# Where the feed-forward of a two-layer kernel turns its next block's tokens: behind a block's first products instead of behind its second ones

## The chip, the core and the metric

The kernel runs on one core of one Trainium2 chip. A core has a matrix engine (TensorE, PE in the profile), three engines for elementwise work (VectorE or DVE, ScalarE or ACT, GpSimd or POOL), a queue that issues transfers (SyncE, SP), and an accumulator memory (PSUM) from which the other engines must fetch what PE has made. Each engine works its own instructions in the order in which they were built, and waits on semaphores for the others. The metric is the time of one execution on the device in microseconds (us).

## The reference, cut to what matters

Tokens are 4 sequences of 1024, each of width 256. Two layers are computed; each has a mixing part and a feed-forward part, each followed by a residual and a layer norm:

```
x = layernorm(x + L0_attn(x))      # state-space mixing, 2 heads of 128
x = layernorm(x + gelu(x @ w1 + b1) @ w2 + b2)   # w1 256x1024, w2 1024x256, exact gelu
x = layernorm(x + L1_attn(x))      # linear attention: exp features of q and k, 16 heads
x = layernorm(x + L1_ffn(x))       # 2 shared experts and 2 of 8 routed experts, silu
```

The change lies in the second line. Its first product makes the 1024 hidden values of a token, its second one brings them back to 256.

## The kernel before, in words

The tokens are cut into 8 blocks (`i`) of 512, each of 4 tiles of 128. All data is float32. A block goes through the state-space part (`ssd_block`), the feed-forward (`ffn_block`), attention and the router in halves of 256 tokens (`attn_front`, `attn_back`, index `hb`, two for each block; `attn_tail`), the shared experts (`shared_jobs`, run as `job`), and last the routed experts (`slot_tiles`), which come after everything else.

**The order on PE is planned while the program is built.** Each stage registers pieces of work as `Task(run, cost, rank, after, pool, banks, hold)`. `trace_tasks` then simulates a single server: again and again it takes the task that can start first, and among those that can start at once the one of lowest rank. A task starts no sooner than `wait` units after the tasks in `after`, and no sooner than its `banks` of PSUM are free in its pool. Pool 0 has six banks and pool 1 has two. The planner's costs are constants in the code. What it writes down is an order of instructions, and the hardware then keeps that order on PE, whatever the waits really last. ACT and DVE get an order that follows from it. While attention, feed-forward and shared experts overlap, low ranks (attention, near 5) go before high ones (feed-forward, 10 and more; shared experts, 100).

**The feed-forward of one block** is nine tasks in pool 1. `turn_x` transposes the block's tokens on PE into two banks; ACT copies both to `xT` (tile of one buffer). `hidden`, four tasks, makes two of the eight slices of hidden values each: four matmuls (eight records in the profile) into two banks, then a GELU for each bank on ACT into `hT` (also one buffer). `outputs`, four tasks for the four tiles, multiplies `hT` with `w2`; each pair shares one bank, and one addition on DVE takes the pair into the residual. The last one is followed by the layer norm. In front of the first, POOL adds the bias `b2` to the residual.

Blocks are taken in the order 0, 2, 1, 3, 4, 5, 6, 7. Each is chained behind the one before: `turn_x` waits until the last `outputs` of the preceding block has been placed (`before`).

**What shares the engines with it.** From block 1 on, attention runs in between. `attn_front` transposes its tokens (`turn_x` of its own, one copy on ACT to `xTa`), makes queries and keys (`project`), transposes these (`turn_qk`, for keys a copy on ACT to `qkT`, for queries one on DVE), and makes the features (`features`, first of the keys, then of the queries): PE fills four banks, and ACT and DVE clip and exponentiate them: two clips on DVE, two relus on ACT (L583), four exponentials on ACT (L581, L584). `attn_back` has `scores` (one ACT copy, a multiplication on POOL, three on DVE), `turn_keys` (two ACT copies to `kt`), `outputs`, `turn`, `turn_back` (ACT copy to `oT`) and `project`. The exponentials, the GELU and the SiLU of the shared experts belong to different function tables of ACT; a table is changed by an instruction ACT_TABLE_LOAD ahead of the next function.

When the last block's `outputs` are done, `open_second` gives the space of the feed-forward's weights to those of the shared experts and loads them; 20 units later the first shared `job` may start. All `job`s use pool 1 while attention runs.

Of the kernel before, what the change touches and what calls it, by code (L numbers as in the profile page):

```python
# [76 lines left out]
def two_layers(ctx: ExitStack, tc: tile.TileContext, x, xT, vecs, cols, wx, w1, w2, wqkv, wout, om, rw, moe, out):  # L77
# [19 lines left out]
    def bank(name, n):  # L97

        return psum[n].tile([P, 512], F32, tag="bank", name=name)
# [100 lines left out]
    def transposed(t, i, tiles, n, engines):  # L200


        width = len(tiles) * P
        engines = list(engines)
        for c0 in range(0, KC, 512 // width):
            chunks = range(c0, min(KC, c0 + 512 // width))
            ps = bank(f"ps_t{t.name}_{c0}", n)
            at = 0
            for c in chunks:
                for j in tiles:  # L210
                    nc.tensor.transpose(ps[:, at : at + P], xs[i][:, j, c * P : (c + 1) * P], ident)
                    at += P
            engines.pop(0)(t[:, c0 : chunks[-1] + 1, :].rearrange("p c t -> p (c t)"), ps[:, :at])
        return t

    def layernorm(i, by_act=False):

        st = sm.tile([P, NT, 6], F32, tag="ln_st", name=f"ln_st{i}")
        mv = sm.tile([P, NT, 2], F32, tag="ln_mv", name=f"ln_mv{i}")
        v = sm.tile([P, NT], F32, tag="ln_v", name=f"ln_v{i}")  # L220
        for j in range(NT):
            nc.vector.bn_stats(st[:, j, :], xs[i][:, j, :])
            nc.vector.bn_aggr(mv[:, j, :], st[:, j, :])
        nc.vector.tensor_scalar_add(v, mv[:, :, 1], LN_EPS)
        r = rsqrt(v, [P, NT], "ln")
        if by_act:
            nc.vector.scalar_tensor_tensor(v, mv[:, :, 0], -1.0, r, ALU.mult, ALU.mult)
            for j in range(NT):
                nc.scalar.activation(
                    xs[i][:, j, :], xs[i][:, j, :], AF.Identity, bias=v[:, j : j + 1], scale=r[:, j : j + 1]  # L230
                )
            return
        for j in range(NT):
            nc.vector.tensor_scalar(
                xs[i][:, j, :], xs[i][:, j, :], mv[:, j, 0:1], r[:, j : j + 1], ALU.subtract, ALU.mult
            )
# [37 lines left out]


    states = [None] * NB
    ssd_end, ffn_end, proj_end, turn_end, tail_end = {}, {}, {}, {}, {}

    def ssd_block(i, wk):

# [153 lines left out]
    def ffn_block(i, before, wk):  # L434
        v = SimpleNamespace(ps=None)

        def turn_x():
            v.xT = wk.tile([P, KC, TB], F32, tag="xT", name=f"xT{i}")
            transposed(v.xT, i, range(NT), 1, (nc.scalar.copy, nc.scalar.copy))
            v.hT = wk.tile([P, HID0 // P, TB], F32, tag="hT", name=f"hT{i}")  # L440

        def hidden(ms):
            for m in ms:
                ps = bank(f"ps_h{i}_{m}", 1)
                for k in range(KC):
                    nc.tensor.matmul(  # L446
                        ps, w1_sb[:, k, m * P : (m + 1) * P], v.xT[:, k, :], start=(k == 0), stop=(k == KC - 1)
                    )
                nc.scalar.activation(v.hT[:, m, :], ps, AF.Gelu, bias=col[:, m : m + 1])  # L449

        def outputs(j):
            if j == 0:
                b2 = vec0[:, _VEC["b2"]].unsqueeze(1).to_broadcast([P, NT, D])
                nc.gpsimd.tensor_add(xs[i], xs[i], b2)
            if j % 2 == 0:
                v.ps = bank(f"ps_f{i}_{j}", 1).rearrange("p (s d) -> p s d", s=2)
            for m in range(HID0 // P):
                nc.tensor.matmul(  # L458
                    v.ps[:, j % 2, :],
                    v.hT[:, m, j * P : (j + 1) * P],  # L460
                    w2_sb[:, m, :],
                    start=(m == 0),
                    stop=(m == HID0 // P - 1),
                )
            if j % 2 == 1:
                nc.vector.tensor_add(xs[i][:, j - 1 : j + 1, :], v.ps, xs[i][:, j - 1 : j + 1, :])
            if j == NT - 1:
                layernorm(i)

        r = 10.0 + i  # L470
        last = Task(turn_x, 0.9, r, [(ssd_end[i], 10.0), (before, 0.0)], 1, 2)
        wait = 4.0
        for n in range(4):
            last = Task(lambda n=n: hidden(range(2 * n, 2 * n + 2)), 3.5, r + 0.1 * n, [(last, wait)], 1, 2, 2.2)
            wait = 0.0
        wait = 3.0
        for j in range(NT):
            last = Task(lambda j=j: outputs(j), 3.5, r + 0.5 + 0.1 * j, [(last, wait)], 1, (j + 1) % 2, 2.2)
            wait = 0.0
        ffn_end[i] = last  # L480
# [676 lines left out]
    with tc.manual_schedule(engines={mybir.EngineType.PE}):  # L1157
# [8 lines left out]
        before = None  # L1166
        ffn_order = [0, 2, 1, 3, 4, 5, 6, 7]
        for i in ffn_order:
            ffn_block(i, before, wkf)
            before = ffn_end[i]  # L1170
        constants = Task(attn_constants, 0.0, 4.0, [(ssd_end[0], 0.0)])
        spaces = SimpleNamespace()

# [32 lines left out]
        last = Task(open_second, 0.0, 0.0, [(ffn_end[ffn_order[-1]], 0.0)])  # L1206
        wait, jobs = 20.0, []
        for i, _, cost, n, banks, _ in shared_jobs(early + amid, None, None, None, banks_of, 2):
            after = [(last, wait), (turn_end[i], 3.0)]
# [3 lines left out]
            last, wait = jobs[-1], 0.0  # L1213
# [31 lines left out]
        wait = 6.0  # L1245
        for _ in range(2 * NTOK // P // 8 + 1):
            sending = Task(lambda: spaces.steps.pop(0)(), 0.0, 0.0, [(sending, wait)])
            wait = 3.6
# [14 lines left out]
    with tc.manual_schedule(  # L1263
# [7 lines left out]
        parts, n = [], -1  # L1271
# [94 lines left out]
```

## Time and profile before

| | |
|---|---|
| median of 3 runs | 1563.77 us (1562.93 to 1565.25) |
| profiled execution, its own time | 1563.55 us |
| its span, first to last instruction | 1561.7 us |
| PE clock that was granted, mean | 0.987 of full |
| VectorE busy | 754.3 us (48%) |
| ScalarE busy | 595.6 us (38%) |
| GpSimd busy | 419.6 us (27%) |
| first feed-forward matmul of block 1 (the first beside attention) | 188.1 us |
| weights of the shared experts issued | 661.3 us |
| first product of the shared experts | 686.8 us |
| first product of the routed experts | 1063.9 us |

The span is 1.85 us shorter than the execution's own time; what lies around it is taken to stay. Matmuls in float32 show as two records each. A row of the timeline gives start, duration, engine, source line, output and inputs, the number of records, and in brackets the idle time ahead of it with the instruction that ended it. A row of the windows gives, for a stretch of time, the length, the busy time of PE, weight loads, DVE, ACT and POOL with their instruction counts, the granted clock, and the share and rate of the transfers.

### The profile page before, as it was taken

What the parts mean: (1) busy time and instruction counts of PE and PEld (TensorE: products, weight loads), DVE (VectorE), ACT (ScalarE), POOL (GpSimd) and SP (SyncE); (2) the same over time, 40 slices, a digit from 0 to 9 for tenths busy, and PEclk for the clock granted to TensorE, in tenths of its full rate; (3) what the DMA queues carried; (4) which work ended last, traced back from release to release, by engine and by line L of the source; (5) the groups of instructions that cost most, each with busy time, mean ns of one, the idle gap of its engine ahead of it and who ended that gap; (6) DMA issues with size and microseconds to landing.
All of it is one profiled execution on the core that took longest, in us unless ns stands there. A gap on an engine that the chain in (4) does not pass through costs nothing. (4 is left out here: it accounts for less than half of the span.)

```text
span 1561.7 us, 25308 instructions
## 1 busy us (share of the span) xinstructions
PE 1492.0 (96%) x9704; PEld 966.5 (62%) x9704; DVE 754.3 (48%) x2322; ACT 595.6 (38%) x1048; POOL 419.6 (27%) x456
## 2 busy tenths in 40 slices
PE   9999989999999989989999999999999999999998
PEld 5666657565757665755665765556666666666554
DVE  6877724764756465575555455122222222222264
ACT  3465374535464635345546411111222222222132
POOL 5723302322122121222110003002444444443100
PEclk9999999999999999999999999999999999999999
DMA  9000000000000000020101052132222222222331
GB/s 329 2 1 1 1 1 1 27 2 1 28 2 21 8 1 28 10 114 1 49 8 55 15 190 114 40 135 44 45 45 47 45 46 46 47 46 35 87 109 54
DMA packets 50197, 73.54 MB, mean 47 GB/s; under 512 B 8448, under 2 KB 42752, under 8 KB 48544
## 3 DMA queue, kind: packets, MB, share of 16 engines
q1 hardware_dynamic: 36128, 52.06, 9.3%
q0 software_dynamic: 13248, 18.17, 7.3%
q8 instruction: 80, 1.31, 0.4%
q10 hardware_dynamic: 704, 1.70, 0.3%
q14 instruction: 37, 0.30, 0.1%
HBM read 45.93 MB, written 25.99 MB: 46 GB/s over the span
## 5 line engine op out<-in xcount | busy, mean ns | idle before, releaser
L1019 PE MATMUL ps_ge<-w,xeT 128*128 x552 | 248.5, 593 | 1.0 <-issue 1.0
L947 PE MATMUL ps_g<-xTs,w 128*128 128x512 f32 x512 | 226.0, 594 | 5.5 <-ACT sl L955 3.0
L947 PEld LDWEIGHTS ps_g<-xTs,w 128*128 128x128 f32 x512 | 95.6, 190 | 119.6 <-issue 105.8
L1019 PEld LDWEIGHTS ps_ge<-w,xeT 128*128 128x128 f32 x552 | 99.5, 190 | 100.6 <-issue 100.6
L1050 POOL DMA_INDIRECT acc<-ye,back x69 | 109.3, 1584 | 110.8 <-DVE xew L1006 76.1
L1029 DVE TENSOR_TENSOR ge<-se,ps_ge 128x512 f32<-128x512 f32 x69 | 47.5, 688 | 178.3 <-PE ps_ge L1019 178.3
L1041 PE MATMUL ps_ye<-w2e,geT 128*128 x552 | 130.7, 380 | 0.9 <-DVE geT L1036 0.9
L446 PE MATMUL ps_h<-xT,w_sb 128*128 128x512 f32 x256 | 124.7, 632 | 5.4 <-ACT hT L449 5.3
L994 POOL DMA_INDIRECT xe<-xt,sent x69 | 68.0, 986 | 228.6 <-PE ps_xe L1002 164.2
L458 PE MATMUL ps_f<-w_sb,hT 128*128 128x256 f32 x512 | 116.2, 380 | 0.8 <-ACT hT L449 0.7
L965 PE MATMUL ps_e<-w,gT 128*128 128x256 f32 x512 | 114.6, 380 | 2.1 <-DVE x L974 2.1
L627 POOL TENSOR_TENSOR sc<-sc,mask_le 128x512 f32<-128x512 f32 x32 | 40.8, 1276 | 277.1 <-ACT sc L626 277.1
L965 PEld LDWEIGHTS ps_e<-w,gT 128*128 128x128 f32 x512 | 96.1, 190 | 18.9 <-DVE x L974 3.7
L1041 PEld LDWEIGHTS ps_ye<-w2e,geT 128*128 128x128 f32 x552 | 99.6, 190 | 12.2 <-ACT ye L1049 1.1
L458 PEld LDWEIGHTS ps_f<-w_sb,hT 128*128 128x128 f32 x512 | 95.5, 190 | 16.8 <-issue 3.4
L956 DVE TENSOR_TENSOR gT<-sl,ps_g 128x512 f32<-128x512 f32 x64 | 43.9, 686 | 114.9 <-PE ps_g L947 94.1
L955 ACT ACTIVATE sl<-ps_g 128x512 f32<-128x512 f32 x64 | 38.1, 597 | 159.2 <-PE ps_g L947 145.6
L446 PEld LDWEIGHTS ps_h<-xT,w_sb 128*128 128x128 f32 x256 | 50.2, 203 | 62.4 <-issue 51.5
L1027 ACT ACTIVATE se<-ps_ge 128x512 f32<-128x512 f32 x69 | 41.3, 599 | 121.5 <-PE ps_ge L1019 121.5
L629 DVE TENSOR_TENSOR sc<-ps_sc,mask_le 128x512 f32<-128x512 f32 x96 | 62.8, 685 | 40.2 <-PE ps_sc L617 33.1
L617 PE MATMUL ps_sc<-qf,kf 64*128 64x128 f32 x1024 | 67.2, 280 | 3.1 <-DVE kf L580 1.2
L617 PEld LDWEIGHTS ps_sc<-qf,kf 64*128 64x128 f32 x1024 | 60.6, 189 | 12.9 <-issue 6.0
(268 smaller groups left out, 2417.0 us busy)
## 6 DMA issues: line engine op xcount, KB each, us to landing
w<-in_moe SPq DMA_DIRECT2D x8, 1024.0 KB, 8.9
x<-in_x SPq DMA_DIRECT2D x8, 512.0 KB, 10.6
xt<-x SPq DMA_DIRECT2D x8, 512.0 KB, 3.6
td<-xTr SPq DMA_DIRECT2D x16, 256.0 KB, 2.5
w2e<-in_moe SPq DMA_DIRECT2D x8, 512.0 KB, 8.0
x<-acc SPq DMA_DIRECT2D x8, 512.0 KB, 7.7
xt<-in_xT SPq DMA_DIRECT2D x7, 512.0 KB, 11.0
out<-x SPq DMA_DIRECT2D x7, 512.0 KB, 2.9
```

What stands on the lines that cost most here:

```text
L446: nc.tensor.matmul(ps, w1_sb[:, k, m * P : (m + 1) * P], v.xT[:, k, :], start=(k == 0), stop=(k == KC - 1))
L458: nc.tensor.matmul(v.ps[:, j % 2, :], v.hT[:, m, j * P : (j + 1) * P], w2_sb[:, m, :], start=(m == 0), stop=(m == HID0 // P - 1),)
L617: nc.tensor.matmul(ps[s][:, r * P : (r + 1) * P], kf[rows, r, q, tok], qf[rows, r, q, tok], start=True, stop=True)
L629: nc.vector.tensor_mul(t_s, ps_s, mask)
L947: nc.tensor.matmul(ps[s], w[e][:, 2 * s + k, m * P : (m + 1) * P], xT[i][:, k, :], start=(k == 0), stop=(k == KC - 1),)
L956: nc.vector.tensor_mul(gT[i, e][:, m, :], sl, ps[1])
L965: nc.tensor.matmul(ps, gT[i, e][:, m, j * P : (j + 1) * P], w2e[:, m, :], start=(e == 0 and m == 0), stop=(e == NSH - 1 and m == HID // P ...
L994: nc.gpsimd.indirect_dma_start(out=xe, out_offset=None, in_=xt, in_offset=bass.IndirectOffsetOnAxis(ap=sent[:, s : s + 1], axis=0),)
L1019: nc.tensor.matmul(pg[a], xeT[s][:, k, :], w13[:, bass.ds(e * (4 * HID) + (2 * a + k) * HID, HID)], start=(k == 0), stop=(k == KC - 1),)
L1029: nc.vector.tensor_mul(ge[s], se, pg[1])
L1041: nc.tensor.matmul(ps[:, :D], geT[s][:, m, :], w2[:, bass.ds(of[s] * (2 * HID) + m * D, D)], start=(m == 0), stop=(m == HID // P - 1),)
L1050: nc.gpsimd.indirect_dma_start(out=acc, out_offset=bass.IndirectOffsetOnAxis(ap=back[:, s : s + 1], axis=0), in_=ye, in_offset=None, compu ...
```

## The change

`turn_x` of a block no longer waits for the last `outputs` of the block before, but for its last `hidden`. It gets a rank lower by 0.8, so that it goes ahead of that block's own remaining feed-forward tasks. The first `hidden` of a block now waits for the last `outputs` of the block before on its own account, since `hT` has one buffer. No instruction of PE is added or removed; the planner is given other constraints, and its whole order after the first change follows from them.

```diff
-        last = Task(turn_x, 0.9, r, [(ssd_end[i], 10.0), (before, 0.0)], 1, 2)
+        last = Task(turn_x, 0.9, r - 0.8, [(ssd_end[i], 10.0), (hid_end.get(before), 0.0)], 1, 2)
         wait = 4.0
         for n in range(4):
-            last = Task(lambda n=n: hidden(range(2 * n, 2 * n + 2)), 3.5, r + 0.1 * n, [(last, wait)], 1, 2, 2.2)
+            after = [(last, wait)] + [(ffn_end.get(before), 0.0)] * (n == 0)
+            last = Task(lambda n=n: hidden(range(2 * n, 2 * n + 2)), 3.5, r + 0.1 * n, after, 1, 2, 2.2)
             wait = 0.0
+        hid_end[i] = last
...
         for i in ffn_order:
             ffn_block(i, before, wkf)
-            before = ffn_end[i]
+            before = i
```

More of the change, by code (lines that the diff above doesn't have):

```diff
@@ L276, in two_layers @@
     states = [None] * NB
-    ssd_end, ffn_end, proj_end, turn_end, tail_end = {}, {}, {}, {}, {}
+    ssd_end, hid_end, ffn_end, proj_end, turn_end, tail_end = {}, {}, {}, {}, {}, {}
     def ssd_block(i, wk):
```

## The prediction

> **What bounds the kernel.** I read the page's first part, then the windows over the stretch in which feed-forward, attention and shared experts overlap, then PE's timeline and its waits there.
>
> ```profile
> PE 1492.0 (96%) x9704; PEld 966.5 (62%) x9704; DVE 754.3 (48%) x2322; ACT 595.6 (38%) x1048; POOL 419.6 (27%) x456
> ```
>
> PE is the bound, and the change adds no matmul. It can only move PE's idle time and the clock that the idle time costs. The next rows show where that is: stretch, length, busy PE; the third number from the end is the granted clock.
>
> ```profile
> 180.00:222.00 42.00, 34.45 (x232) 20.20 (x230) 19.54 (x48) 30.92 (x42) 5.33 (x4) 0.92 0.00 0
> 262.00:316.00 54.00, 50.81 (x315) 31.81 (x307) 34.68 (x107) 27.75 (x43) 19.42 (x19) 1.00 0.07 21
> 316.00:362.00 46.00, 41.49 (x395) 27.85 (x394) 27.49 (x67) 21.98 (x40) 9.60 (x9) 0.93 0.00 1
> 362.00:446.00 84.00, 80.64 (x782) 55.79 (x781) 51.71 (x148) 44.40 (x76) 19.57 (x19) 0.98 0.04 14
> 446.00:545.00 99.00, 94.13 (x944) 65.78 (x946) 54.72 (x152) 51.90 (x87) 19.88 (x20) 1.00 0.04 12
> 545.00:640.00 95.00, 84.05 (x798) 58.33 (x788) 55.25 (x149) 43.95 (x75) 21.32 (x21) 0.95 0.04 12
> ```
>
> With 222:262 (2.69 us idle), 640:680 (5.66) and 680:860 (8.15) PE idles 50.9 us between 180 and 860; after that until 1060 it hardly idles. Summed over the same windows, length times (1 - clock) is 16 us of lost clock. By the waits, ACT ends 34.9 us of the idle time and DVE 15.8.
>
> **How ACT makes PE wait: one place worked out.** This is PE, then ACT, in block 7 of before:
>
> ```profile
> 525.22 1.15 PE L570 MATMUL ps_p<-qkT,om_sb 32*128 32x256 f32 x16
> 526.78 3.60 PE L446 MATMUL ps_h<-xT,w_sb 128*128 128x512 f32 x8
> 535.14 0.66 PE L639 MATMUL ps_k<-ident,kf 128*128 128x128 f32 x4 [1.95 <-ACT xTa L213]
> ...
> 526.42 0.69 ACT L583 ACTIVATE qf<-ps_p,fcap 128x512 f32<-128x512 f32 x1 [0.87 <-PE ps_p L570]
> 527.13 1.28 ACT L581 ACT_TABLE_LOAD   x1
> 528.42 0.72 ACT L581 ACTIVATE qf<-qf,fbias 128x512 f32<-128x512 f32 x1
> 532.05 1.28 ACT L449 ACT_TABLE_LOAD   x1
> 533.35 1.27 ACT L449 ACTIVATE hT<-ps_h,col 128x512 f32<-128x512 f32 x2
> 534.50 0.59 ACT L213 COPY xTa<-ps_txTa 128x512 f32<-128x512 f32 x1
> ```
>
> Counted from the start of the features on PE: the first relu starts at 1.2, a load takes 1.28, exponentials start 0.62 apart, a relu 0.67, a copy 0.57. So relu 1.9, load 3.2, three exponentials 5.1, relu 5.7, copy 6.3, exponential 6.9, load 8.2, two GELUs 9.4, copy of xTa 9.9. PE has queued features, turn_qk, hidden, turn_qk, turn_x, features, half of turn_keys: done at 8.0. It should wait 1.9; the row says 1.95. I use this count for the new order.
>
> **The change part by part.**
>
> *Table loads.* In the program as built, ACT holds 82 loads before and 94 after: 27 to 31 ahead of GELUs, 24 to 29 ahead of exponentials, 12 to 14 ahead of SiLUs, one more in the state-space part. At 1.283 us that is 15.4 us of ACT, mostly because `hidden` now falls between the key and the query features. ACT then runs exponential, load, GELU, load, exponential, load, GELU, load ("split"). Before has two splits with GELUs (blocks 1 and 3), after has four (1, 5, 6, 7). The Trainium skill (ScalarE: Activation LUTs, "What ACT_TABLE_LOAD costs") puts a switch at about 2.66 us, of which 1.38 is a drain. Here no drain shows: the load at 532.05 ends at 533.33 and the GELU starts at 533.35. By the page's figure 12 loads are an estimated 32 us, and the wait just worked out, with two loads in it, would be 4.7 and not 1.95. I take 1.28.
>
> *Block 6 in the new order.* PE: key features, project (0.98), hidden, query features, two turn_qk (0.9), hidden, attention's turn_x, key features, turn_keys, hidden, scores (2.0), the router's turn_x (0.9), the moved turn_x. ACT: relu 1.9, load, three exponentials 5.1, relu 5.8, load, GELU 7.7, load, exponential 9.7, load, GELU 11.7, load, then relus, exponentials and the copy of qkT to 16.8. PE comes to the second half of hidden at 9.6 and waits for that second GELU's bank: 2.2. At 14.3 it wants qkT: 2.5. Then the copy of xTa: 1.9. The moved turn_x comes 2.9 us behind a hidden whose GELUs stand behind a load and the key exponentials: 1.2. The attention's outputs wait for the scores' copy behind those GELUs and POOL's mask (1.28): 0.7; logits 0.74, as at 512.9 before. Sum 9.2; before 4.9 (446:545).
>
> *The other blocks, counted the same way.* Block 1 with the first two turns: its split 6.5 (0.6, 2.2, 3.1, 0.6), the moved turn_x for block 3 with scores and advance 2.3, the turns for blocks 2 and 1 0.9: 9.7, against 10.2. Block 3: no split, GELUs in one run, turn_back no longer right behind turn: 1.0, against 3.2. Block 4: `turn_x` for block 5 stands right behind key features, and its first copy on ACT behind relu, load, three exponentials and a relu, at 5.6; PE is at 2.0, and outputs needs that bank: 3.5, against 4.5. Block 5: the copy of oT stands behind the split, project waits 2.9; xTa 1.8, turn_x 1.1, outputs 0.7: 6.5, against 3.4. Block 7: 2.0, 2.2, 1.9, 1.2 and logits 0.74: 8.0, against 10.95 (its 4.94 for oT and 2.10 for a GELU go). The hole between the feed-forward's end and the shared experts is shorter of waits: one turn_back 0.2 us behind its turn, 3.0 (2.69 in the like place at 258.2), against 5.66. Shared experts with attention, one split more: 9.3, against 8.15.
>
> After: 9.7+1.0+3.5+6.5+9.2+8.0+3.0+9.3 = 50.2, against 50.9. But the count follows ACT and leaves out DVE except in the hole and one 0.75. Of before's 15.8 us that DVE ends, 12 are of kinds not counted. DVE's work is unchanged, the places are new. Bounds: 0 (all gone) and 12 (all come back elsewhere); no row decides, I take the middle, 6. So idle time 56, **+5.3 us**.
>
> *Clock.* The Trainium skill (TensorE: Matmul & The Clock Gate, "HAM oscillation") warns of idle gaps over about 3.4 us. By that, only before's 4.94 and after's 3.5 would cost clock, about even. The trace is harsher: after the wait of 2.10 at 619.3 a hidden took 5.40 us for its 3.60. So waits near 2 count. Before has nine of 1.8 or more for 16 us; after has twelve, but packed as in 180:222, where several lose 3.4 together. Block by block 3.4 (block 1), 1.8, 2, 3.4, 3.4, 1.8 make 15.8: **no difference**. If each costs 16/9 = 1.8, +5.4.
>
> *Costed at nothing.* The moved copies and transposes are as many as before. SP: the shared weights wait for the feed-forward's last matmuls either way, and the first shared product came 25 us later (661.3 to 686.8); the plan keeps 22 units. The dispatch ends at 1010.9 and the routed experts start at 1063.9; some 12 units of shared work move ahead of it, so some 40 of 53 us of cover stay; POOL's gathers and the routed weights stay covered. If the cover were gone, the dispatch's remainder would be bare, but it isn't near.
>
> Total 1563.55 + 5.3 = **1569 us**, 5.2 over the median, which itself lies 0.2 above the profiled execution.
>
> **Rivals.**
> 1. *Slower by more* (0.20): every long wait costs its own clock, +5.4, and DVE's uncounted waits come back halfway beyond my 6, +3: 1577. For it: 619.3. Against: 535.1, where 1.95 cost no clock.
> 2. *No change* (0.18): DVE's waits are mostly gone with the tight places (turn_back at 258, the 2.51 at 344.9): 1564.
> 3. *Faster* (0.27): the splits are hidden. The one in block 3 of before cost only 0.63+0.59+0.74 = 2.0, since outputs, which ask nothing of ACT, stood behind it. If those of blocks 5, 6 and 7 cost 2.0 each and not 2.9, 4.7 and 4.2, 5.8 go, and if DVE's 6 don't come either: 50.2-5.8 = 44.4 of idle time, 1557. It decides from a split cost of 3.1 down, with DVE's share nil (50.2-11.8+3x3.1 = 47.7, 3.2 below before). Against: behind these splits stands another hidden, which needs the late bank.
> The forecast itself (0.35): 1569. That the order doesn't change as said is excluded by the built order: each turn_x stands ahead of the preceding block's outputs.
>
> **Range**: 1556 (the faster rival and 1 us) to 1579 (the slower one and 2). What a measurement can tell from no change is 0.2%, 3.1 us. Faster by over that 0.27, within 0.18, slower 0.20+0.35 = 0.55. The slower cases alone: 1566 to 1579.
>
> **What would show it.** ACT loads up by 12 and ACT busy up about 15 us. In blocks 5 to 7, waits of 2 to 3 us of hidden for a GELU, of features for qkT, and of project for oT; 3.5 us ahead of outputs of block 4. No 4.94 wait. If splits show waits under 2 us in sum, the third rival is right; if DVE ends less than 8 us, the second; if clock loss passes 20 us, the first.

## The result, and the profile after

The changed kernel takes 1575.74 us (median of 6 runs, 1571.35 to 1581.68) against 1563.24 us before (6 runs, 1561.79 to 1565.25): a ratio of 1.0083, 95% interval 1.0057 to 1.0110. It is slower, by 12.5 us. Its profiled execution took 1572.48 us, 8.9 more than that of before; its span is 1570.6.

The page's first part, and then the windows (length, busy PE, weight loads, DVE, ACT and POOL, granted clock, transfers). The stretches from 222 to 262 and from 640 to 680, not shown, had the full clock:

```profile
PE 1492.1 (95%) x9704; PEld 966.9 (62%) x9704; DVE 751.5 (48%) x2322; ACT 610.8 (39%) x1060; POOL 419.6 (27%) x456
```

```profile
180.00:222.00 42.00, 34.77 (x219) 22.25 (x218) 23.36 (x61) 31.06 (x42) 6.61 (x7) 0.96 0.00 1
262.00:316.00 54.00, 52.03 (x243) 33.78 (x241) 32.66 (x106) 20.70 (x35) 18.22 (x16) 1.00 0.06 20
316.00:362.00 46.00, 38.65 (x377) 25.02 (x378) 21.73 (x55) 18.50 (x33) 10.82 (x10) 0.91 0.01 1
362.00:446.00 84.00, 75.93 (x726) 53.53 (x725) 45.12 (x126) 48.50 (x77) 14.76 (x13) 0.95 0.04 14
446.00:545.00 99.00, 91.42 (x922) 62.30 (x922) 56.77 (x161) 50.72 (x83) 22.33 (x23) 0.97 0.04 12
545.00:640.00 95.00, 87.32 (x814) 62.26 (x813) 56.85 (x172) 52.32 (x84) 18.45 (x19) 0.98 0.04 12
680.00:860.00 180.00, 172.05 (x1612) 113.55 (x1614) 99.27 (x260) 98.52 (x161) 28.06 (x30) 0.96 0.08 25
```

PE's busy time is the same to 0.1 us, so the 8.9 us are idle time of PE. ACT has 12 instructions and 15.2 us more: the table loads. Cut by the work instead of by the clock (the shared experts' part ends some 8 us later than before), PE's idle time is 2.9 us where 0.3 was between 95 and 180 us, 53.3 where 50.9 was in the overlap (180 to 860, now to 868), and 4.4 where 0.5 was from there to the routed experts: +2.6, +2.4 and +3.9. Length times (1 - clock), summed over the windows from 180 to 860, is 22 us, where it was 16.

Two places stand out among the new waits. In block 4, the turn for block 5 stands right behind the key features. First PE, after a like row from an earlier stretch, then ACT, then DVE there:

```profile
108.91 3.72 PE L458 MATMUL ps_f<-w_sb,hT 128*128 128x256 f32 x16 [0.61 <-ACT xT L213]
...
349.00 1.15 PE L573 MATMUL ps_p<-qkT,om_sb 32*128 32x256 f32 x16
350.08 1.09 PE L211 MATMUL ps_txT<-ident,x 128*128 128x128 f32 x8
358.07 6.43 PE L458 MATMUL ps_f<-w_sb,hT 128*128 128x256 f32 x16 [6.90 <-ACT xT L213]
```

```profile
350.91 1.28 ACT L584 ACT_TABLE_LOAD   x1
355.03 0.72 ACT L584 ACTIVATE kf<-kf,fbias 128x512 f32<-128x512 f32 x1 [2.84 <-DVE kf L583]
355.66 0.70 ACT L587 ACTIVATE kf<-kf,ecap 128x512 f32<-128x512 f32 x1
...
356.89 0.67 ACT L586 ACTIVATE kf<-ps_p,fcap 128x512 f32<-128x512 f32 x1
357.46 0.57 ACT L213 COPY xT<-ps_txT 128x512 f32<-128x512 f32 x1
```

```profile
351.54 1.76 DVE L520 TENSOR_SCALAR ss<-ss 128x64 f32<-128x64 f32 x1
...
354.05 0.22 DVE L192 TENSOR_TENSOR qkn_s<-qkn_s,ss 128x64 f32<-128x64 f32 x1
354.19 0.80 DVE L583 TENSOR_SCALAR kf<-ps_p,fcap,ffloor 128x512 f32<-128x512 f32 x1
```

Read from the bottom: DVE has the norm of the next queries and keys ahead of the clip of the key features (the operation that limits their values before the exponential), so the clip starts at 354.19. ACT had its exponential table in place at 352.2 and waits 2.84 us for that clip. The copy of `xT` stands behind three exponentials and a relu, at 357.46. PE was through with the turn at 351.2, needs the bank of `xT` for `outputs`, and idles 6.90 us. Then its clock is low: it was granted at 0.50 from 353.4, inside the wait, to 363.6, and the sixteen records of `outputs` take 6.43 us, where the row at 108.91 takes 3.72.

The second place lies outside the overlap. PE and DVE beside the dispatch, whose comparisons are the rows of `in_tile` and `in_lane`:

```profile
969.59 3.18 PE L968 MATMUL ps_e<-w,gT 128*128 128x256 f32 x14
976.11 4.15 PE L968 MATMUL ps_e<-w,gT 128*128 128x256 f32 x18 [3.33 <-DVE gT L959]
```

```profile
971.51 1.22 DVE L894 TENSOR_TENSOR in_lane<-lane_no,lane 128x1024 f16<-128x1024 f32 x1
972.65 1.67 DVE L886 TENSOR_TENSOR in_tile<-tile_no,its 128x568 f16<-128x568 f32 x1
974.25 1.21 DVE L894 TENSOR_TENSOR in_lane<-lane_no,lane 128x1024 f16<-128x1024 f32 x1
975.38 0.67 DVE L959 TENSOR_TENSOR gT<-sl,ps_g 128x512 f32<-128x512 f32 x1
```

The shared experts' product `gT` stands on DVE behind the dispatch's comparisons. Before, the same comparisons began beside second products (`ps_e`), which ask less of DVE than the first ones (`ps_g`): one operation of 0.7 us for 7 us of products, where those have one for 3.4. The like wait was 0.45 us:

```profile
928.79 7.15 PE L965 MATMUL ps_e<-w,gT 128*128 128x256 f32 x32
935.78 19.05 PE L947 MATMUL ps_g<-xTs,w 128*128 128x512 f32 x44
955.27 8.85 PE L947 MATMUL ps_g<-xTs,w 128*128 128x512 f32 x20 [0.45 <-DVE gT L956]
...
933.62 0.73 DVE L883 TENSOR_TENSOR in_tile<-tile_no,its 128x568 f16<-128x568 f32 x1
```

The splits are there as forecast. In block 7:

```profile
586.84 1.98 PE L446 MATMUL ps_h<-xT,w_sb 128*128 128x512 f32 x4 [1.34 <-ACT hT L449]
590.88 2.41 PE L446 MATMUL ps_h<-xT,w_sb 128*128 128x512 f32 x4 [2.05 <-ACT hT L449]
```

Such a pair of waits of `hidden` stands in blocks 1, 6 and 7, and a project waits 3.56 us for `oT` in block 5.

### The profile page after: what moved, and what is told of

Same layout as the page of the kernel before. It is cut to its first block, busy times and chain, and to the rows that moved or that the text cites. A ratio compares the mean times of both kernels' runs of the same rounds, so it can differ in the third digit from the quotient of the medians.

```text
span 1570.6 us, 25318 instructions
## 1 busy us (share of the span) xinstructions
PE 1492.1 (95%) x9704; PEld 966.9 (62%) x9704; DVE 751.5 (48%) x2322; ACT 610.8 (39%) x1060; POOL 419.6 (27%) x456
## 5 line engine op out<-in xcount | busy, mean ns | idle before, releaser
L446 PE MATMUL ps_h<-xT,w_sb 128*128 128x512 f32 x256 | 120.0, 609 | 12.4 <-ACT hT L449 10.3
L446 PEld LDWEIGHTS ps_h<-xT,w_sb 128*128 128x128 f32 x256 | 47.0, 193 | 63.7 <-issue 44.8
L1052 ACT ACTIVATE ye<-ps_ye,xew 128x256 f32<-128x256 f32 x69 | 32.7, 474 | 92.6 <-PE ps_ye L1044 92.6
L1007 ACT COPY xeT<-ps_xe 128x256 f32<-128x256 f32 x69 | 25.8, 374 | 106.5 <-PE ps_xe L1005 106.5
## 6 DMA issues: line engine op xcount, KB each, us to landing
x<-in_x SPq DMA_DIRECT2D x8, 512.0 KB, 10.8
```

The costliest lines, as they stand in the source:

```text
L446: nc.tensor.matmul(ps, w1_sb[:, k, m * P : (m + 1) * P], v.xT[:, k, :], start=(k == 0), stop=(k == KC - 1))
```

## The experiments

Each is compared by its ratio to the kernel before, from runs on the same chip. Six of them only edit the order of the planned tasks. For this the plan is first made whole, then edited, then built:

```diff
-            task.run()
+            order.append(task)
...
+        for task in order:
+            task.run()
```

Four theories stood at the start. *Splits*: the added table loads between key and query features make the loss. *Turn*: an early `turn_x` waits for its own banks and copies. *Order*: it is the plan that was made anew, not the place of the turn. *Dispatch*: its comparisons now meet other shared products.

### The turn without the new plan, and the new plan without the turn

The plan of before, with each turn moved right ahead of the preceding block's first `outputs`:

```diff
+        for one, two in zip(blocks, blocks[1:]):
+            order.remove(turns[two])
+            order.insert(order.index(firsts[one]), turns[two])
```

> The plan of before is kept task by task, and only each turn_x is taken out of its place and put right ahead of the preceding block's first outputs: the turn moved, without the new order. ACT keeps 82 table loads. Theory 'order' (the loss is in the new order: hidden between key and query features, 12 more table loads): at most 4 us above before, 1563 to 1567. Theory 'turn' (the moved turn itself costs, since its copies stand behind ACT's queue and hold pool 1's two banks in front of outputs; in after these waits sum to 12.0 us: 0.61, 1.40, 1.38, 0.34, 6.90, 1.34): 8 us or more above before, 1571 or later.

The plan of the changed kernel, with each turn put back behind the preceding block's last `outputs`:

```diff
+        for one, two in zip(blocks, blocks[1:]):
+            order.remove(turns[two])
+            order.insert(order.index(ffn_end[one]) + 1, turns[two])
```

> The counterpart: after's plan is kept task by task, and only each turn_x is put back right behind the preceding block's last outputs. ACT keeps 94 table loads. Theory 'order': within 4 us of after, 1571 to 1577, with the waits of hidden for a GELU (2.05 each) and of features for qkT still there in blocks 5 to 7. Theory 'turn': the 6.90 us wait and the turn's other waits go, about 1564 to 1566, less some 2 us each where hidden now follows its turn at once (block 4).

| ratio to the kernel before | turn behind the second products | turn ahead of them |
|---|---|---|
| plan of before | 1 | 1.0127 (1.0112 to 1.0141), 1582.11 us |
| plan of the changed kernel | 1.0085 (1.0072 to 1.0098), 1574.81 us | 1.0083 (1.0057 to 1.0110), 1575.74 us |

Both halves cost by themselves, and they do not add up: the new plan costs some 13 us with either place of the turn. With the turn early in the old plan, PE shows where the time goes:

```profile
301.13 0.66 PE L211 MATMUL ps_txT<-ident,x 128*128 128x128 f32 x4
305.16 1.12 PE L211 MATMUL ps_txT<-ident,x 128*128 128x128 f32 x4 [3.38 <-ACT hT L456]
311.30 2.93 PE L465 MATMUL ps_f<-w_sb,hT 128*128 128x256 f32 x6 [5.02 <-ACT xT L213]
```

The turn's second half waits for a bank that a GELU still holds, and `outputs` then waits for the turn's copy, which ACT has behind a set of exponentials. Waits of 4.08 and 4.95 us of the same kind follow in later blocks. With the turn late in the new plan, the 6.90 us wait is gone, but the turns wait 5.9 us in six places for the residual's addition on DVE, other waits come up (attention's state 5.3 us, a mask on POOL 2.7), and the 3.33 us at the dispatch and the 3.56 for `oT` stay. So the early turn is not needed for the loss, and it makes one of its own in the old plan. The splits are all in the new plan with either place of the turn, so this pair does not tell whether they or the places make the new plan's loss.

### No hidden between key and query features

A rule is added to the planner of the changed kernel: no `hidden` while key features are placed and their query features are not. Table loads fall from 94 to 76, fewer than the 82 of before.

```diff
+                if task.table and any(k.end is not None and q.end is None for k, q in pairs):
+                    continue
```

> After with one rule more in the planner: a hidden may not be placed while a half's key features are placed and its query features are not. 76 table loads in place of 94. Theory 'order', if the splits are what costs: the 2.05 us waits of hidden for a GELU in blocks 5 to 7, the 2.9 in block 1 for qkT and the 3.56 for oT go, 1562 to 1567. Theory 'turn': the turn's waits stay, 1572 or later. Theory 'luck' (any new order moves the time by some 8 us either way, whatever the loads): no value is excluded, but loads and time then go different ways.

It took 1592.95 us, 1.0195 (1.0182 to 1.0208): the fewest loads of any kernel that keeps the GELU, and the longest time of all. The rule makes yet another plan, and in it two turns stand right behind features, with waits of 8.27 and 4.27 us ahead of `outputs`; `scores` waits 10.5 us for DVE. So the number of loads does not order the times. It is no clean test of the splits, since the plan moved with the rule.

### The loads themselves: a relu in place of the GELU

This keeps each kernel's PE order and takes away the loads of `hidden`; the values that come out are no longer the reference's.

```diff
-                nc.scalar.activation(v.hT[:, m, :], ps, AF.Gelu, bias=col[:, m : m + 1])
+                nc.scalar.activation(v.hT[:, m, :], ps, AF.Relu, bias=col[:, m : m + 1])
```

> The kernel before, with a relu in place of the GELU in the feed-forward's hidden values (so the output is not the reference's): ACT needs no table for hidden, 28 loads stay of 82, PE's order is that of before. Both theories: ACT busy falls by about 54 x 1.28 = 69 us; the waits of hidden for a GELU behind a load shrink, some 10 us of the 35 that ACT ends go, about 1550 us. This run is the base for the like edit of the changed kernel.

> The changed kernel with the same relu (output not the reference's): 32 loads stay of 94, PE's order is that of the changed kernel. Theory 'splits' (the change's loss is table loads between key and query exponentials): the distance to the like edit of before falls from 12.5 us to 3 or less. Theory 'places' (the loss is what the new order puts side by side, copies behind feature work and DVE, and the dispatch's wait, whatever the loads): the distance stays at 8 or more; the 6.90 us wait ahead of block 4's second products and the 3.3 us wait for gT stay.

Before with a relu: 1536.80 us (0.9844, 0.9830 to 0.9857). Changed with a relu: 1547.58 us (0.9909, 0.9894 to 0.9924). The distance is 10.8 us, where it was 12.5: the theory *places* holds. The loads are dear in both kernels: 25.0 us of gain in the one, where some 12 had been expected, and 28.2 in the other. What the change loses by having more of them is 1.7 us by the two distances and 2.8 by the ratios, and the intervals do not tell either from nothing. The wait in block 4 stays without the GELU's loads:

```profile
343.94 6.12 PE L458 MATMUL ps_f<-w_sb,hT 128*128 128x256 f32 x16 [6.91 <-ACT xT L213]
```

The 3.33 us at the dispatch stay too.

### One turn moved

The changed kernel, with the turn for block 5 alone put ahead of the key features that stood in front of it:

```diff
+        order.remove(turns[5])
+        order.insert(order.index(key_feats[3]), turns[5])
```

> The changed kernel, with the turn for block 5 alone moved ahead of the key features of half 3, everything else in the changed kernel's order (94 loads). Theory 'the copy stands behind the key features on ACT': the 6.90 us wait ahead of block 4's second products falls to about 1.3, and the clock after it recovers: 5 to 7 us less than the changed kernel, about 1569. Theory 'the two banks are late whatever stands before': the wait stays above 4 and the time within 3 us of the changed kernel.

It took 1565.12 us, 1.0029 (1.0018 to 1.0039), more gain than expected. PE and ACT in block 4:

```profile
347.56 1.04 PE L211 MATMUL ps_txT<-ident,x 128*128 128x128 f32 x8
348.53 1.15 PE L581 MATMUL ps_p<-qkT,om_sb 32*128 32x256 f32 x16
349.61 3.72 PE L463 MATMUL ps_f<-w_sb,hT 128*128 128x256 f32 x16
```

```profile
348.20 1.07 ACT L213 COPY xT<-ps_txT 128x512 f32<-128x512 f32 x2 [4.00 <-PE ps_txT L211]
```

The copies now go on an idle ACT, 0.1 us behind the turn's first half; no wait, full clock from 347 to 360, and 3.72 us for `outputs`. Two small waits for the features come in, 0.28 and 0.83. The account closes: 6.90 of wait and 6.43 - 3.72 = 2.71 of clock, less 1.11, is 8.5 us; the two profiled executions differ by 8.4, and so do the ratios (0.0054 of 1563). One turn, 1.1 us of PE's work, moved by one task, is two thirds of the loss. DVE's part in the wait, the 2.84 us for the clip, is read from the rows; no run changes it alone.

The same edit in the plan of before with early turns, for three of them:

```diff
+        for two, ahead_of in ((4, query_feats[2]), (5, query_feats[4]), (7, key_feats[8])):
+            order.remove(turns[two])
+            order.insert(order.index(ahead_of), turns[two])
```

> The kernel before's order with each turn ahead of the preceding block's second products (1582 us), and with the turns for blocks 4, 5 and 7 put ahead of the features that stood just in front of them (82 loads). Theory 'the copy stands behind features on ACT': the waits of 3.4+5.0, 4.1 and 5.0 us behind these turns shrink to under 1.5 each, and the time falls by some 13 us to about 1569. Theory 'an early turn costs wherever it stands': above 1577.

1566.81 us, 1.0026 (1.0015 to 1.0037), from 1.0127. The waits of `outputs` for the copy (5.02, 4.08, 4.95) are all gone or 0.24. Not all went as expected: the turn for block 4 still waits 3.61 and 3.24 us for banks held by GELUs in a split, and that for block 7 2.83. The place is confirmed a second time; the early turn's other wait, for its banks, is a cost of its own.

### The dispatch

First try: the dispatch's steps 5.6 units apart in the planner, not 3.6.

```diff
-            wait = 3.6
+            wait = 5.6
```

> After with the dispatch's DVE steps spaced 5.6 planner units apart in place of 3.6; the order of PE up to there stays. If the 3.33 us wait at 976 us (outputs of a shared block for a product on DVE, behind the dispatch's comparisons) is part of the loss: 3 to 5 us under after, 1570 to 1573, and that wait is gone. If the dispatch only ends later and bares the start of the routed experts: no gain or a loss.

1572.35 us, 1.0065 (1.0052 to 1.0078); the wait is still 3.34 us. DVE's order did not follow the planner's spacing, so this tested nothing, although the time fell where the first theory had put it. Second try, on top of the moved turn: open_routed and the steps behind it each seven tasks later, so that the comparisons begin beside second products, as they did before.

```diff
+        steps = [(order.index(t), t) for t in sent_off]
+        for at, t in reversed(steps):
+            order.remove(t)
+            order.insert(at + 7, t)
```

> The changed kernel with the turn for block 5 ahead of the key features (as before, 1565.1 us) and, new, the dispatch's steps each seven tasks later, so that its comparisons on DVE begin beside the shared experts' second products instead of beside six first ones. Theory 'gT stands behind the comparisons': the 3.33 us wait near 968 shrinks under 1, about 3 us less, 1562. Theory 'the dispatch's later end comes bare': PE waits ahead of the routed experts and the time is 1565 or more.

1562.17 us (14 runs), 1.0003 (0.9995 to 1.0011): the time of the kernel before. The wait:

```profile
963.53 14.06 PE L982 MATMUL ps_e<-w,gT 128*128 128x256 f32 x64
977.43 12.18 PE L964 MATMUL ps_g<-xTs,w 128*128 128x512 f32 x28
990.02 5.42 PE L964 MATMUL ps_g<-xTs,w 128*128 128x512 f32 x12 [0.42 <-DVE gT L973]
```

3.33 became 0.42, and the median is 2.95 less (the ratio 1.0003, from 1.0029); the later end of the dispatch, at 1049.1, still lies ahead of the routed experts at 1064.2. With two places mended, all splits and all 94 loads still in, the loss is gone: PE idles 69.6 us of the span, and 69.7 before. Other waits still differ between these two kernels; they balance.

### Other plans of the same tasks

The kernel before, with the planner's cost of `hidden` 3.6 in place of 3.5, and nothing else:

```diff
-            last = Task(lambda n=n: hidden(range(2 * n, 2 * n + 2)), 3.5, r + 0.1 * n, [(last, wait)], 1, 2, 2.2)
+            last = Task(lambda n=n: hidden(range(2 * n, 2 * n + 2)), 3.6, r + 0.1 * n, [(last, wait)], 1, 2, 2.2)
```

> The kernel before, with the planner's cost of hidden 3.6 in place of 3.5 and nothing else: the turn stays behind the preceding block's last product, but the plan is made anew from the first places where attention and feed-forward compete (88 table loads). Theory 'any fresh plan of these tasks falls some 10 us short of the plan of before': 1568 or more. Theory 'the loss comes with the early turn': 1559 to 1565.

1579.07 us, 1.0111 (1.0096 to 1.0125), with no early turn at all. Its waits of PE from 180 to 1060 (us in total, times, longest):

```profile
PE ps_p L570 <- ACT qkT L557: 12.4, 7, 3.8
PE ps_h L446 <- ACT hT L449: 12.1, 9, 2.1
PE ps_oT L714 <- DVE o L707: 7.2, 3, 3.0
```

In before these rows are 7.1, 5.3 and 3.1 us; in the changed kernel 8.3, 9.6 and 3.8. And the changed kernel with the turn's rank not lowered:

```diff
-        last = Task(turn_x, 0.9, r - 0.8, [(ssd_end[i], 10.0), (hid_end.get(before), 0.0)], 1, 2)
+        last = Task(turn_x, 0.9, r, [(ssd_end[i], 10.0), (hid_end.get(before), 0.0)], 1, 2)
```

> The changed kernel with the turn's rank left at that of its block (only what it waits for is changed), which gives a third plan (86 table loads). Theory 'the plan decides': it lies 4 us or more away from the changed kernel's 1575.7, on either side. Theory 'the early turn costs its own amount whatever the plan': within 3 us of it.

1570.03 us, 1.0049 (1.0036 to 1.0062): the same early turn, another plan, some 5 us less, though the two intervals overlap. A tenth of a unit in one cost moves the kernel before by as much as the change did. So a loss of this size needs no early turn, only another plan.

### A version that beats both

On top of the version with the moved turn and the later dispatch, three more consumers go behind work that asks nothing of ACT or DVE (in the text on record, "the run before last" is that version):

```diff
+        put(at_tile[7]["w"], query_feats[4], 3)
+        put(at_tile[18]["oT"], at_tile[19]["o"])
+        put(at_tile[18]["w"], at_tile[18]["oT"], 3)
+        put(at_tile[25]["w"], query_feats[13], 3)
```

`put(a, b, n)` places task a as the n-th behind b; "w" is attention's project, "oT" its turn_back, "o" its outputs.

> The kernel of the run before last (turn for block 5 ahead of the key features, dispatch later; 1562.2 us), with three more consumers moved behind work that asks nothing of ACT: attention's project of the second tile of halves 3 and 12 three tasks later, turn_back and project of half 9's first tile behind the next outputs and values. Theory 'a wait for a late copy is worth what stands ahead of it': the waits of 3.55 (402 us), 2.27 (649) and 2.19 (797) go or fall under 0.5, 5 to 8 us less, 1555 to 1557, the first to beat the kernel before. Theory 'ACT's work sets the pace there, and the wait comes back at the next consumer': above 1560.

1553.67 us, 0.9951 (0.9939 to 0.9963). The changed kernel at the first of these places, then this one:

```profile
401.61 2.74 PE L510 MATMUL ps_qk<-wqkv_sb,xTa 128*128 128x512 f32 x6
407.91 2.04 PE L724 MATMUL ps_w<-wout_sb,oT 128*128 128x256 f32 x4 [3.56 <-ACT oT L719]
```

```profile
398.33 1.15 PE L594 MATMUL ps_p<-qkT,om_sb 32*128 32x256 f32 x16
399.91 0.66 PE L579 MATMUL ps_qkT<-ident,qk 128*128 128x128 f32 x4 [0.43 <-DVE qk L534]
400.40 3.60 PE L464 MATMUL ps_h<-xT,w_sb 128*128 128x512 f32 x8
403.84 1.03 PE L747 MATMUL ps_w<-wout_sb,oT 128*128 128x256 f32 x4
```

The features, which ACT was waiting for, now start ahead of the project that waited for ACT, and the 3.55 us do not come back: behind this place, 1.12 and 0.98 us of wait stand where the version without these moves has 1.30, 0.26 and 1.62. The 2.27 near 649 is gone. The 2.19 near 797 comes back in part: waits of 1.73, 0.88 and 1.17 us stand behind it there.

## Why the prediction was right, and where it was not

The forecast was 1569 us, slower, by idle time of PE. The profiled execution came to 1572.5, the median to 1575.7. The direction and the kind of loss were right; the size was not: 12.5 us over the median of before, where 5.2 was forecast, and nearer to the first rival's 1577 than to 1569. Point by point:

- **Table loads**: +12 and +15.2 us of ACT, as worked out. But where the forecast's count rises above before (blocks 5 and 6, the shared experts), it rises by splits, and the relu pair and the version at 1562.17 show that the splits are not the net loss: they cost about what the waits they displaced had cost (4.94 for `oT` and 2.10 for a GELU are gone, as forecast).
- **The count by block**: block 1 8.8 forecast without its first turns, 7.2 measured; block 3 1.0 and 0.3; block 4 3.5 and 9.0; block 5 6.5 and 8.1; block 6 9.2 and 7.6; block 7 8.0 and 7.7; the hole 3.0 and 2.4; the shared experts with attention 9.3 and 11.0. The turns for blocks 2 and 1, ahead of 180 us, came to 2.7 for 0.9. The measured figures hold waits for DVE too.
- **The step that failed**: "outputs needs that bank: 3.5", in block 4. The mechanism was right and the size was not: 6.90 us, and 2.7 of clock behind it. The 5.6 in the count is where the copy starts, not where it ends, 0.57 later; and the count took ACT's queue alone, so it left out that the exponentials would wait 2.84 us for a clip that DVE had behind the norm of the next queries and keys. 3.5 + 0.57 + 2.84 is the 6.9. A `hidden` that waits 2.08 us in the same block for the residual's addition was in no block's count.
- **The 6 us for DVE**: no row decided it. Between 95 and 868 us DVE ends 8.5 us of PE's waits (15.9 before), and 2.4 of them lie in the hole, which the count held; the other 6.0 are what the 6 stood for. That is luck. So is most of the agreement of the sum, 56.2 forecast and 56.0 measured with the first two turns: block 4 and the first turns came out over, blocks 1, 3 and 6 under.
- **"Costed at nothing", the dispatch**: its end stayed covered, as said, but not its comparisons. I asked who covers the dispatch and not what it stands in front of on DVE. 3.33 us there (0.45 before) and 1.06 at 886 are the miss of the profiled execution.
- **Clock**: "no difference" did not hold by the forecast's own sum, 22 us of lost clock for 16. From 680 to 860 alone it is 7 us, with none before. PE's busy time is nevertheless the same to 0.1 us; part of the low clock lay inside waits, as from 353.4 to 358.1. The median run lies 3.3 us above the profiled one, and the six runs go from 1571.35 at a granted clock of 0.986 to 1581.68 at 0.977; before's lie within 3.5. So clock is in the median in part.
- **The rivals**: "slower by more" named lost clock over 20 us as its sign, and that came; its other half, more waits for DVE, did not. "Faster" asked for splits of 2 us. The pairs of waits in blocks 6 and 7 alone are 3.2 and 3.4, and with the wait for `qkT` behind them 4.8 and 4.2, as counted; so no. "No change" fell with the two places, and would have been right without them.

## What to carry to other kernels

When a plan is made anew from a changed constraint, the change's own effect is lost in the draw: build the order, find the one or two longest new waits, and move the waiting task by one place before judging the idea. In this kernel, a copy that must free a bank belonged ahead of a batch of exponentials, or its consumer behind work that asks nothing of that engine. Follow a wait one engine further than the row names: here PE's wait for ACT was in good part ACT's wait for DVE.

## What the runs showed of the hardware

The clock's answer to a wait is not the same each time. After waits of 6.90, 6.91, 8.27, 4.27, 4.86, 5.02 and 4.08 us, sixteen records of `outputs` took 6.43, 6.12, 5.81, 5.97, 6.78, 5.16 and 6.55 us instead of 3.72. After a wait of 2.05 us, four records of `hidden` took 1.98 us at one place of the changed kernel (204.55) and 2.48 and 2.41 at two others (502.19, 590.88), and 3.41 at the first of these places in the version with the rank left. So waits near 2 us sometimes cost clock, and those of 4 us and more ahead of `outputs` did each time.

The records right behind a wait do not tell all of it. In the changed kernel the clock between 180 and 860 us is either full or 0.50, and 0.50 for 3.41 us or two or three times that; behind the wait at 204.55 it fell at 210.0 only, after the next wait, of 2.90. The version with the dispatch's steps 5.6 apart has the same order there as the changed kernel; at its two later places the four records took 1.98 us, and the clock fell at 507.1 and 595.9 instead of 503.5 and 592.3. So one order can meet the low clock at other places in another execution. The changed kernel's times lie 10 us apart from run to run, before's 3; that its waits near 2 us make this was not tested, and the old plan with early turns, with eight waits of 2 us or more, lies within 0.8 in four runs.
